# Letting attention steps wait for their PSUM bank in the clock model of a gated cross-attention and expert kernel

## The chip, the cores and the metric

The kernel runs on one core of a Trainium2 chip. The metric is the device time of one execution in microseconds (us), as the median of several executions. The profiler records one execution; its span runs from the first to the last recorded instruction, and the execution's own time is a little longer than its span. The engines are TensorE (PE, with its weight loads as PEld), VectorE (DVE), ScalarE (ACT), GpSimd (POOL) and SyncE (SP), which here only issues DMAs and waits.

## The reference

Four batches of 2048 rows of width 512 go through two gated layers. `context` has 128 rows for each batch. Everything is in float32.

```python
def layernorm(x): return (x - mean(x)) / sqrt(var(x) + 1e-5)        # over the last axis

def xattn(query, ref):                                              # ref: 128 rows
    Q, K, V = query @ Wq + bq, ref @ Wk + bk, ref @ Wv + bv
    return (softmax(Q @ K.T) / sqrt(512)) @ V

def ffn(x):                                                         # one expert for a batch
    e = argmax(mean(x, rows) @ Wr + br)                             # of 8
    return relu(x @ W1[e] + b1[e]) @ W2[e] + b2[e]                  # 512 -> 2048 -> 512

x = x + tanh(g_xattn) * xattn(layernorm(x), context)
x = x + tanh(g_ffn) * ffn(layernorm(x))
```

## The kernel before

**Attention.** Rows are taken in 16 blocks of 512, four for each batch. Since `Q @ K.T` is `layernorm(x) @ (Wq @ K.T)` plus a bias, the kernel makes `M = Wq @ K.T` and `V` once for each batch (`keys`, `values`), and a block needs `x @ M` alone. The generator `attention` issues one block in steps: row statistics on DVE and POOL (tiles `st`, `mv`, `ve`, `rstd`), the scores `psc` on PE, softmax on DVE and ACT (`sc`, `nmax`), transposes `pp`, then four products `pav` with `V` (L288). DVE adds each of these to the rows (L276, `added`). Statistics are made again, ACT normalises (`xT`, L303, after DVE's `shift`, L297), PE transposes the result in four pieces `pt` (L335), and ACT copies each of them out with a column sum (L322, `copied`). The sums go into the mean that picks the expert.

`pav` and `pt` alternate between two small pools of PSUM banks, `ps_a` and `ps_t`. Blocks 0 to 2 share pools with two banks each; block 3 and all blocks of later batches have one bank in each pool. So the third `pav` of a later block needs the bank of the first, which DVE's add gives back, and the third `pt` needs ACT's first copy.

**Feed-forward.** Each layer's product is cut into quarters twice and done with 7 products in place of 8 at either level (49 in place of 64); the sums of blocks that this needs are made by DVE and POOL. For the weights they are made once for each batch and half of the hidden width: SP loads the expert's blocks (`base`, `home`, L593 and L599), POOL and in the first half also DVE sum them (L564), SP stores the sums to DRAM (`W1d`, `W2d`, L585), and a ring of four large and two small tiles `w` takes them back (L777 to L790). The first four groups of the first stage use the sums where they are made. There are 16 stages (4 batches, 2 pairs of blocks, 2 halves of the hidden width); all products are issued by `chain` (L811) into banks `X`, `Y` and `Q`.

**Who sets the order.** Nothing is reordered on the chip's queues by the program at run time: the order in which the Python code issues instructions is the order of each engine's queue. That order comes from generators and a clock model. A generator yields what its last instructions cost, as pairs such as `("DVE", 0.76)`. `Stream.step` adds these up. A step may yield two chains; the stream goes on at the end of the first one (`at`), and remembers the end of the latest in `later`. A step that yields the word `"join"` sets `at` to `later`.

The kernel has two parts. Up to the feed-forward (the prologue), the next stream is always the one with the smallest `at`, and a `filler` (`others`, the keys and values of batches 1 to 3) is put in wherever the model's PE is free before that. After it, the feed-forward's own steps call `tick`, which lets the stream `slow` (attention of later batches and their routing) and the stream `staged` (weight sums) take as many steps as a credit allows (`paced`, `PACE`), if their `at` is no more than 1.4 us ahead.

The steps of `pav` and `pt` yield two chains: PE's time, then the time of the add on DVE or the copy on ACT. The bank counter `held` is lowered when the add or copy is issued, not when the model has it done.

```python
            if t - 1 in pav:
                added(t - 1)
            yield (("PE", 0.87 * (t < 4)),), (("DVE", 0.76 * (t > 0)),)
```

Other places that matter: `route` (zm, zb, `pr` L521, `ei`, L539) picks a batch's expert and only then can SP load its weights; `begin` (L1302) are six small products of zeros on the feed-forward's banks, the first of that part; the last rows are stored by `store` (L1137), which is called by the table `after`.

Of the kernel before, what the change touches and what calls it, by code (L numbers as in the profile page):

```python
# [89 lines left out]
def flamingo(tc, ctx, x, xT, cxT, g_x, g_f, WqT, Wk, Wv, bqk, bv, Wr, br, W1, b1, W2, b2, out):  # L90
    nc = tc.nc
    B, N, H = x.shape
# [8 lines left out]
    Q = 2 * P  # L101
# [74 lines left out]
    def room(ps):  # L176
        while held[ps] == ROOM[ps]:
            yield (("DMA", 0.3),)
        held[ps] += 1
# [16 lines left out]
    def attention(b, blk, pools):  # L196
# [84 lines left out]
        for t in range(5):  # L281
            if t < 4:
                ps, tag = ((ps_a, "pa"), (ps_t, "pt"))[t % 2]
                if held[ps] == ROOM[ps] and t - 1 in pav:
                    added(t - 1)
                yield from room(ps)
                pav[t] = ps.tile([P, H], F32, tag=tag, name="pav"), ps
                nc.tensor.matmul(  # L288
                    pav[t][0], lhsT=pT[:, t * P : (t + 1) * P], rhs=Vb, start=True, stop=True
# [4 lines that stand above are left out]
# [33 lines left out]
        for kc in range(KC + 1):  # L327
            if kc < KC:
                ps, tag = ((ps_t, "pt"), (ps_a, "pa"))[kc % 2]
                if held[ps] == ROOM[ps] and kc - 1 in pt:  # L330
                    copied(kc - 1)
                yield from room(ps)
                pt[kc] = ps.tile([P, TB], F32, tag=tag, name="pt"), ps
                for t in range(4):
                    nc.tensor.transpose(  # L335
                        pt[kc][0][:, t * P : (t + 1) * P], z[:, t, kc * P : (kc + 1) * P], ident
                    )
            if kc - 1 in pt:
                copied(kc - 1)
            yield (("PE", 0.45 * (kc < KC)),), (("ACT", 0.8 * (kc > 0)),)  # L340
# [44 lines left out]
    if True:  # L385
        M0 = mvp.tile([P, KC, S], F32, tag="M", name="M_0")
        V0 = mvp.tile([P, H], F32, tag="V", name="V_0")
        ctxT0, KT0 = in_home(stp, "tt", (1, KC, S), (KC, S), n=21 * P)
        ctxTr = sp.tile([P, B - 1, KC, S], F32, name="ctxTr")
        w = {name: sp.tile([P, KC, H], F32, name=f"w{name}") for name in ("k", "q", "v")}  # L390
        bvb = sp.tile([P, H], F32, name="bvb")
        KTr, V3 = in_home(hp, "s2", (KC, (B - 1) * S), (H,))
        Ms = sp.tile([P, B - 1, KC, S], F32, name="Ms")
        Vs, ready_kv = {}, set()
        order = [(b, blk) for b in range(B) for blk in range(NBLK)][:EARLY]
        streams = [
            attention(*i, (*homes[n], *three) if n < 3 else one) for n, i in enumerate(order)
        ]
        nc.sync.dma_start(ctxT0, cxT[:, 0:1])
        for c in range(KC):  # L400
            nc.sync.dma_start(w["k"][:, :, c * P : (c + 1) * P], Wk[:, :, c * P : (c + 1) * P])
        with nc.allow_non_contiguous_dma(reason="bias"):
            nc.scalar.dma_start(bvb, bv.partition_broadcast(P))
        nc.sync.dma_start(w["q"], WqT)
        next(streams[0])
        nc.sync.dma_start(w["v"], Wv)
        nc.sync.dma_start(ctxTr, cxT[:, 1:B])

        def keys(cT, n, KT, M, pc_out):

            took = 0.43 * n + 0.02

            def sums(name, left, right):
                yield from room(ps_k)
                p = ps_k.tile([P, n, S], F32, tag="pk", name=name)
                for k in range(KC):
                    nc.tensor.matmul(  # L417
                        p, lhsT=left(k), rhs=right(k), start=k == 0, stop=k == KC - 1
                    )
                    if k % 2:  # L420
                        yield (("PE", took),)
                return p

            for m in range(KC):
                pk = yield from sums(
                    "pk", lambda k: w["k"][:, k, m * P : (m + 1) * P], lambda k: cT[:, :, k, :]
                )
                nc.vector.tensor_scalar(
                    KT[:, m, :], pk.rearrange("p n s -> p (n s)"), bqk_t[:, KC + m : KC + m + 1],
                    None, ALU.add,  # L430
                )
                held[ps_k] -= 1
                yield (("DVE", 0.5),)
            for kc in range(KC):
                pm = yield from sums(
                    "pm", lambda m: w["q"][:, m, kc * P : (kc + 1) * P], lambda m: KT[:, m, :]
                )
                nc.scalar.copy(M(kc), pm)
                held[ps_k] -= 1
                yield (("ACT", 0.5),)  # L440
            pc = yield from sums("pc", lambda m: bqk_t[:, m : m + 1].to_broadcast([P, P]), lambda m: KT[:, m, :])
            nc.scalar.copy(pc_out, pc.rearrange("p n s -> p (n s)"))
            held[ps_k] -= 1
            yield (("ACT", 0.5),)

        def values(cT, V):
            yield from room(ps_k)
            pv = ps_k.tile([P, H], F32, tag="pk", name="pv")
            for kc in range(KC):
                nc.tensor.matmul(  # L450
                    pv, lhsT=cT[:, kc, :], rhs=w["v"][:, kc, :], start=kc == 0, stop=kc == KC - 1
                )
                if kc % 2:
                    yield (("PE", 1.72),)
            nc.vector.tensor_tensor(V, pv, bvb, ALU.add)
            held[ps_k] -= 1
            yield (("DVE", 0.75),)

        def own():

            yield (("DMA", 11),)
            first_keys = keys(ctxT0, 1, KT0, lambda kc: M0[:, kc : kc + 1, :], cq[:, 0:S])
            for _ in range(12):
                yield next(first_keys)
            for m in range(KC):
                st = small.tile([P, 6], F32, tag="st", name="st", bufs=4)
                mq = small.tile([P, 2], F32, tag="mq", name="mq", bufs=2)
                nc.vector.bn_stats(st, w["q"][:, m, :])
                nc.vector.bn_aggr(mq, st)
                nc.vector.tensor_scalar(  # L470
                    w["q"][:, m, :], w["q"][:, m, :], mq[:, 0:1], None, ALU.subtract
                )
                yield (("DVE", 1.3),)
            yield from first_keys
            MV[0] = [M0, None]
            yield from values(ctxT0[:, 0], V0)
            MV[0][1] = V0

        def others():

            for lo, hi in ((1, 2), (2, B)):
                at = slice(lo - 1, hi - 1)
                yield from keys(
                    ctxTr[:, at], hi - lo, KTr[:, :, (lo - 1) * S : (hi - 1) * S],
                    lambda kc: Ms[:, at, kc, :], cq[:, lo * S : hi * S],
                )
                for b in range(lo, hi):
                    Vs[b] = V3 if b == 3 else sp.tile([P, H], F32, name=f"V_{b}")
                    yield from values(ctxTr[:, b - 1], Vs[b])
                    ready_kv.add(b)  # L490
                    if b > 1:
                        nc.sync.dma_start(Md[b], Ms[:, b - 1, :, :])
                        nc.sync.dma_start(Vd[b], Vs[b])
            yield from until(lambda: 1 in MV)

        def second_batch():

            yield from until(lambda: 1 in ready_kv and all((0, i) in done_at for i in range(NBLK)))
            Mb = mvp.tile([P, KC, S], F32, tag="M", name="M_1")
            Vb = mvp.tile([P, H], F32, tag="V", name="V_1")  # L500
            nc.scalar.copy(Mb, Ms[:, 0])
            nc.scalar.copy(Vb, Vs[1])
            MV[1] = [Mb, Vb]
            yield (("ACT", 1.2),)
# [232 lines left out]
    NS = B * NF * 2  # L737
# [213 lines left out]
    Ys = {}  # L951
# [165 lines left out]
    def ffn2(b, blk, fh, half):  # L1117
# [15 lines left out]

        def store(cp, i):
            if fh:
                o = slice(2 * cp, 2 * cp + 2)
                nc.sync.dma_start(rows(out, b, 2 * blk + i)[:, o, :], Ys[i][:, o, :])  # L1137

        def add(cp, j, v):
            i, m = divmod(j - 11, 10)  # L1140
# [27 lines left out]
        def both(j, cp):  # L1168
# [6 lines left out]
            (2, 0): [(s4, 0), (both, 21, 0)], (2, 1): [(s4, 1), (both, 22, 0)],  # L1175
            (5, 0): [(both, 21, 1)], (5, 1): [(both, 22, 1)],
            (4, 0): [(store, 0, 1), (bias, 0)], (4, 1): [(store, 1, 1)],
            (3, 0): [(store, 0, 0)], (3, 1): [(store, 1, 0)],
        }
        groups = group(0), group(1)  # L1180
        for q in ORDER2:
# [21 lines left out]
    ctx.enter_context(tc.manual_schedule())  # L1203


    BUSY = {"PE": 1.0, "DVE": 1.3, "ACT": 1.3, "POOL": 1.0, "DMA": 1.1, "Q": 1.1, "POW": 4.0, "GAP": 1.0}

    class Stream:
        def __init__(self, gen, at):
# [196 lines left out]
```

## Time and profile before

| | us |
|---|---|
| median of 3 executions (1743.45 to 1746.9) | 1745.74 |
| the profiled execution's own time | 1742.86 |
| its span | 1741.1 |
| PE busy in the span | 1686.3 (97%) |
| DVE, POOL, ACT busy | 1048.7, 654.6, 581.9 |
| `begin` waits, then the feed-forward starts at | 121.9 |
| last add of `y` on DVE starts at | 1736.82 |

A line of instructions gives the start, the busy time, engine, line, operation, `out<-in`, forms and count, and in square brackets the engine's idle time before it with what ended that idle time. A line of stretches gives the stretch, its length, the busy time of PE, PEld, DVE, ACT and POOL with the number of instructions, then PEclk, the share of full TensorE clock that was granted, and DMA use. A line of waits gives who waited for whom, the sum, how often, and the longest.

### The profile page before, as it was taken

Reading aid. Unit: us, or ns where it says so; the run is one execution under the profiler, and the core shown is the slowest. Engines: PE = TensorE matmul, PEld = TensorE weight load, DVE = VectorE, ACT = ScalarE, POOL = GpSimd, SP = SyncE. Lnnn points to the kernel's source line nnn. Section 1 sums busy time; section 2 is a strip of 40 time slices with the busy share of each in tenths; the row PEclk is TensorE's granted clock in tenths of the full one; section 3 lists DMA queues with packets and bytes.
Section 4 is the critical chain, followed back from the end, with each engine's and each line's share of the span. In section 5 each row is a group of like instructions: output and inputs, shape, how many; then the busy total and the mean of one; then the engine's idle time right before and its main releaser. Section 6 shows DMA issues by size and latency. Waiting matters only on the chain.

```text
span 1741.1 us, 21919 instructions
## 1 busy us (share of the span) xinstructions
PE 1686.3 (97%) x7965; PEld 1439.3 (83%) x7966; DVE 1048.7 (60%) x1663; ACT 581.9 (33%) x1284; POOL 654.6 (38%) x536
## 2 busy tenths in 40 slices
PE   6889999999999999998999999999999999999999
PEld 5667788888888888787878788888888888888887
DVE  5756576556666674757648565583846464746362
ACT  1524225253251614514144252322323242414150
POOL 0365424420648621366156520576514210331010
PEclk8989999999999999999999999999999999999999
DMA  7267777465687965478769564679744543545242
GB/s 296 97 255 287 280 259 287 157 237 190 247 324 259 356 235 178 156 284 299 288 244 344 193 229 142 228 276 318 292 150 155 164 160 101 180 145 174 91 136 80
DMA packets 143067, 381.87 MB, mean 219 GB/s; under 512 B 10480, under 2 KB 40176, under 8 KB 128624
## 3 DMA queue, kind: packets, MB, share of 16 engines
q1 hardware_dynamic: 136912, 342.43, 55.9%
q10 hardware_dynamic: 6048, 38.04, 5.5%
q8 instruction: 64, 1.05, 0.2%
q14 instruction: 43, 0.35, 0.1%
HBM read 262.99 MB, written 117.44 MB: 219 GB/s over the span
## 4 chain that ended last, share of the span: by engine, by line
PE 86%; DVE 6%; DMA 4%; issue 1%; ACT 1%; POOL 1%; SPq 0%; DVEq 0%; POOLq 0%; ACTq 0%
PE Y L811 34%; PE Q L811 23%; PE X L811 21%; DMA w<-W1d 3%; PE pav L288 2%; PE psc L234 2%; PE pt L335 1%; DVE st L214 1%; DMA home<-in_W_dram 1%; PE pm L417 1%; PE pv L450 1%; DVE x L276 1%; DVE c L1009 1%; PE pk L417 0%; DMA wq<-in_WqT_dram 0%
## 5 line engine op out<-in xcount | busy, mean ns | idle before, releaser
L811 PE MATMUL Y<-z,w 128*128 128x256 f32 x1296 | 322.8, 382 | 18.0 <-DMA w<-W1d 8.8
L811 PEld LDWEIGHTS Y<-z,w 128*128 128x128 f32 x1296 | 242.7, 190 | 65.2 <-DVE Q L1063 12.8
L978 ACT ACTIVATE h<-c,b1T 128x256 f32<-128x256 f32 x512 | 229.5, 500 | 86.8 <-DVE c L1009 37.1
L564 POOL TENSOR_TENSOR base<-base 128x512 f32<-128x512 f32 (+1 forms) x126 | 183.5, 1462 | 175.5 <-DMA base<-in_W_dram 171.2
L830 ACT COPY Y<-X 128x512 f32<-128x512 f32 x144 | 82.2, 571 | 467.6 <-PE X L811 467.2
L811 PE MATMUL Y<-w,h 128*128 128x256 f32 x1024 | 228.8, 380 | 0.0
L811 PE MATMUL X<-w,h 128*128 128x256 f32 x1024 | 227.9, 379 | 0.0
L811 PE MATMUL Q<-w,h 128*128 128x256 f32 x1024 | 226.9, 379 | 0.0
L811 PEld LDWEIGHTS X<-w,h 128*128 128x128 f32 x1024 | 193.9, 190 | 29.0 <-issue 3.1
L811 PEld LDWEIGHTS Y<-w,h 128*128 128x128 f32 x1024 | 194.7, 191 | 28.1 <-issue 2.0
L811 PEld LDWEIGHTS Q<-w,h 128*128 128x128 f32 x1024 | 194.3, 190 | 26.2
L811 PE MATMUL Q<-z,w 128*128 128x256 f32 x864 | 212.1, 385 | 1.3
L811 PE MATMUL X<-z,w 128*128 128x256 f32 x864 | 207.4, 379 | 0.0
L811 PEld LDWEIGHTS Q<-z,w 128*128 128x128 f32 x864 | 164.8, 193 | 28.6 <-issue 4.2
L1000 POOL TENSOR_TENSOR r<-r,cg 128x512 f32<-128x512 f32 x32 | 40.6, 1270 | 390.3 <-DVE cg L1081 388.4
L811 PEld LDWEIGHTS X<-z,w 128*128 128x128 f32 x864 | 163.5, 190 | 24.8 <-issue 3.3
L564 POOL TENSOR_TENSOR z<-z 128x256 f32<-128x256 f32 x156 | 129.0, 851 | 37.4 <-DVE z L564 33.6
L220 POOL TENSOR_TENSOR rstd<-ve,mhalf 128x4 f32<-128x4 f32 x32 | 34.9, 1089 | 279.1 <-DVE ve L219 279.0
L811 PE MATMUL Y<-w,s 128*128 128x256 f32 x512 | 113.6, 379 | 0.0
L1142 DVE SCALAR_TENSOR_TENSOR y<-Y,gf,y 128x512 f32<-128x512 f32 x64 | 47.8, 746 | 103.1 <-PE Y L811 101.9
L811 PEld LDWEIGHTS Y<-w,s 128*128 128x128 f32 x512 | 96.8, 190 | 12.9
L1142 DVE SCALAR_TENSOR_TENSOR y<-X,gf,y 128x512 f32<-128x512 f32 x32 | 23.9, 746 | 135.3 <-issue 70.7
(145 smaller groups left out, 2081.9 us busy)
## 6 DMA issues: line engine op xcount, KB each, us to landing
w<-W1d SPq DMA_DIRECT2D x108, 512.0 KB, 4.3
w<-W1d SPq DMA_DIRECT2D x108, 384.0 KB, 4.4
w<-W2d SPq DMA_DIRECT2D x64, 512.0 KB, 7.2
base<-in_W_dram SPq DMA_DIRECT2D x29, 1024.0 KB, 8.5
W1d<-base SPq DMA_DIRECT2D x14, 1792.0 KB, 9.3
w<-in_W_dram SPq DMA_DIRECT2D x48, 512.0 KB, 5.1
W1d<-tt SPq DMA_DIRECT2D x14, 1344.0 KB, 6.0
xT<-in_xT_dram SPq DMA_DIRECT2D x16, 1024.0 KB, 10.9
```

What stands on the lines that cost most here:

```text
L214: nc.vector.bn_stats(st, xt[:, t, :])
L220: nc.gpsimd.tensor_tensor(rstd, ve, mhalf, ALU.pow)
L234: nc.tensor.matmul(psc[:, t, :], lhsT=xTt[:, kc, t * P : (t + 1) * P], rhs=Mb[:, kc, :], start=kc == 0, stop=kc == KC - 1,)
L276: nc.vector.scalar_tensor_tensor(xt[:, t, :], t_, coef[:, t : t + 1], xt[:, t, :], ALU.mult, ALU.add)
L288: nc.tensor.matmul(pav[t][0], lhsT=pT[:, t * P : (t + 1) * P], rhs=Vb, start=True, stop=True)
L335: nc.tensor.transpose(pt[kc][0][:, t * P : (t + 1) * P], z[:, t, kc * P : (kc + 1) * P], ident)
L564: eng.tensor_tensor(o, l, r, ALU.subtract)
L811: nc.tensor.matmul(bank[:, c, :], lhsT=left(k, c), rhs=right(k, c), start=fresh and c == 0 and k == 0, stop=c == 1 and k == ks - 1, skip_g ...
L830: nc.scalar.copy(t["Y"], t["X"])
L978: nc.scalar.activation(h[ij][:, v, 2 * m + c, :], src[:, c, :], AF.Relu, bias=b1T[:, f + c : f + c + 1],)
L1000: eng.tensor_tensor(r[j], r[j], v, ALU.add)
L1142: nc.vector.scalar_tensor_tensor(o, v, gf, o, ALU.mult, ALU.add)
```

## The change

Three places, and numbers in a table.

1. In `attention`, the third and fourth `pav` and the third and fourth `pt` are preceded by a `"join"`: in the model, the step that needs a bank back goes on only when the add or copy that was issued before it is done. On the chip the instructions stay the same; their place in the queues moves. Each block has four steps more.
2. In `keys`, the copy of a piece of `M` out of PSUM is issued on ACT or DVE, whichever the model has free first.
3. In the last stage, the rows that are finished last are stored in two column halves. The left columns are stored ahead of the others by the new `store_left`.
4. In the table `BUSY`, factors for DVE, ACT and POW are other numbers.

```diff
@@ attention
                 if held[ps] == ROOM[ps] and t - 1 in pav:
                     added(t - 1)
+                if t > 1:
+                    yield "join"
                 yield from room(ps)
                 pav[t] = ps.tile([P, H], F32, tag=tag, name="pav"), ps
...
                 if held[ps] == ROOM[ps] and kc - 1 in pt:
                     copied(kc - 1)
+                if kc > 1:
+                    yield "join"
                 yield from room(ps)
                 pt[kc] = ps.tile([P, TB], F32, tag=tag, name="pt"), ps
@@ keys
-                nc.scalar.copy(M(kc), pm)
+                name = min(("ACT", "DVE"), key=lambda n: free[n])
+                (nc.scalar.copy if name == "ACT" else nc.vector.tensor_copy)(M(kc), pm)
                 held[ps_k] -= 1
-                yield (("ACT", 0.5),)
+                yield ((name, 0.5),)
@@ ffn2
         def store(cp, i):
             if fh:
-                o = slice(2 * cp, 2 * cp + 2)
-                nc.sync.dma_start(rows(out, b, 2 * blk + i)[:, o, :], Ys[i][:, o, :])
+                o, c = slice(2 * cp, 2 * cp + 2), slice(Q * (s == NS - 1 and i == 0), H)
+                nc.sync.dma_start(rows(out, b, 2 * blk + i)[:, o, c], Ys[i][:, o, c])
+
+        def store_left(cp):
+            if s == NS - 1:
+                o, c = slice(2 * cp, 2 * cp + 2), slice(0, Q)
+                nc.sync.dma_start(rows(out, b, 2 * blk)[:, o, c], Ys[0][:, o, c])
...
-            (3, 0): [(store, 0, 0)], (3, 1): [(store, 1, 0)],
+            (3, 0): [(store_left, 0), (store_left, 1), (store, 0, 0)], (3, 1): [(store, 1, 0)],
@@ the clock model
-    BUSY = {"PE": 1.0, "DVE": 1.3, "ACT": 1.3, "POOL": 1.0, "DMA": 1.1, "Q": 1.1, "POW": 4.0, "GAP": 1.0}
+    BUSY = {"PE": 1.0, "DVE": 1.0, "ACT": 1.0, "POOL": 1.0, "DMA": 1.1, "Q": 1.1, "POW": 1.5, "GAP": 1.0}
```

As built, the changed program has the same matrix products. Three of the twelve copies of `M` pieces move from ACT to DVE, four sums of `z` blocks (128x256) move from DVE to POOL, and two stores are added. The order of the queues is another one from the first `pav` on, in the prologue and in nearly every attention block after it.

## The prediction

> **What bounds the kernel now.** I read the page first, then busy time by stretch, then who PE waits for in each stretch, then the queues around the waits.
>
> ```profile
> 0.00:28.00 28.00, 14.39 (x75) 13.48 (x76) 12.35 (x33) 2.81 (x8) 1.86 (x9) 0.82 0.90 334
> 28.00:122.00 94.00, 83.33 (x426) 61.00 (x426) 67.76 (x156) 34.03 (x97) 39.47 (x34) 0.95 0.42 163
> 122.00:185.00 63.00, 56.49 (x249) 47.06 (x247) 36.38 (x57) 27.31 (x61) 36.69 (x25) 0.92 0.84 321
> 185.00:1737.00 1552.00, 1532.13 (x7220) 1317.77 (x7220) 931.60 (x1419) 517.72 (x1119) 576.60 (x469) 1.00 0.62 217
> 1737.00:1741.10 4.10, 0.00 (x0) 0.00 (x0) 0.56 (x1) 0.00 (x0) 0.00 (x0) 0.91 0.31 128
> ```
>
> PE is the bound, and its work does not change. What can be won is idle time and slow clock: 13.6 us idle up to 28, 10.7 in the prologue from 28 to 122, 6.5 from 122 to 185, 19.9 in the remaining 1552 us, 4.1 at the end. The column PEclk adds 0.05 x 94 = 4.7 us of lost clock in the prologue and 0.08 x 63 = 5.0 after it.
>
> PE's waits from 28 to 122, then from 185 to 1737:
>
> ```profile
> PE pv L450 <- ACT Ms L438: 2.9, 1, 2.9
> PE begin L1302 <- DVE home L455: 2.8, 1, 2.8
> PE pr L521 <- DVE zb L515: 2.1, 1, 2.1
> ```
>
> ```profile
> PE Y L811 <- DMA w<-W1d: 5.3, 4, 2.1
> PE Y L811 <- DVE Q L1063: 4.6, 6, 2.1
> PE pav L288 <- DVE x L276: 3.7, 2, 3.1
> PE pt L335 <- ACT x L322: 2.9, 8, 0.4
> ```
>
> The change aims at the last two lines and at the prologue's queue order. The prologue's three waits, on PE and on the engine it waits for:
>
> ```profile
> 76.11 1.06 PE L417 MATMUL pc<-home,bqk_t 128*128 128x128 f32 x8
> 80.10 5.40 PE L450 MATMUL pv<-wv,ctxTr 128*128 128x512 f32 x8 [2.93 <-ACT Ms L438]
> 95.28 1.85 PE L521 MATMUL pr<-wr,zb 128*128 128x8 f32 x8 [2.14 <-DVE zb L515]
> 118.70 0.38 PE L1302 MATMUL begin<-zero 128*128 128x512 bf16 x1
> 121.90 1.33 PE L1302 MATMUL begin<-zero 128*128 128x512 bf16 x4 [2.82 <-DVE home L455]
> ```
>
> ```profile
> 78.38 1.52 ACT L303 ACTIVATE xT<-x,shift,rstd 128x512 f32<-128x512 f32 x2 [1.87 <-DVE shift L297]
> 91.45 0.48 DVE L428 TENSOR_SCALAR home<-pk,bqk_t 128x256 f32<-128x256 f32 x1 [3.15 <-PE pk L417]
> 94.23 0.90 DVE L515 COPY zb<-zm 128x512 f32<-128x512 f32 x1
> 115.86 5.38 DVE L564 TENSOR_TENSOR tt<-base,tt 128x896 f32<-128x896 f32 x2
> 121.17 0.68 DVE L455 TENSOR_TENSOR home<-pv,bvb 128x512 f32<-128x512 f32 x1
> ```
>
> ACT, in queue order, holds `Ms` behind `xT`, which waits for block 3's `shift`: PE has nothing from 77.17 to 80.10, and runs the next eight `pv` in 5.40 us, where 3.45 is usual. ACT's last copy of `pt` ends at 90.7, but DVE stands before the `home` copy that waits for PE until 91.45, then makes `z` sums, so `zb` is ready only at 95.13. From `zb` hang the expert's number, the loads of its weights (issued at 99.98), DVE's sums of them, and behind these sums, in DVE's queue, the last `V`, for whose bank `begin` waits until 121.9.
>
> **Part by part.** *The prologue's joins.* I follow the new queue orders with the durations of these rows. Up to DVE's first `coef` (42.5) all is as before, and DVE is full from 36 to 68. From there to block 3's `shift` its work is 33.6 us less 1.75 idle, plus 0.25 for an `Ms` copy: 32.1. In the new order I count some 3.7 us of waits on it (0.3 for `psc`, 1.0 for `pav` of block 1, 1.2 for block 2's fourth `pav`, which stands behind `pp` of block 3, 1.2 for the last `rstd`), so `shift` starts at 78.3, against 76.04. It took 2.30 us before, beside POOL's first `z` sum, and that sum again starts with it: 80.6 against 78.35. But ACT has by then done all of blocks 0 and 1 and three of four `xT` of block 2; left are 5 `xT` (0.75), one small copy and 8 copies of 0.58: 89.2 against 90.7. PE waits some 2 us for block 2's last `xT`, as it waited 2.93.
>
> Behind the last copy DVE now has `zm` and `zb` at once, since only the first half of the `home` copies stands ahead and its products are issued before the last `pt`: `zb` at 90.9 in place of 95.13. The loads go out 4.5 to 5 us after the `pr` products and the seven small steps to `ei`, as before: 94.5 against 99.98. The eight `base` sums follow 5.5 us after that; then come DVE's three `tt` (1.5, 2.7, 2.7), `base` (2.4), four `z` (0.7 each) and two `V` (0.6): the last `V` at 116.8 against 121.85. PE itself is through with `pv` at 110.4 by its work, so it waits 6 us there and starts slow, as before. **Term: -5.1.** Bounds: if DVE's chain did not hold, PE's own work would allow 112 with some slow clock, -9; if ACT's or DVE's waits cost 5 us more than I counted, nothing is won, 0.
>
> *From 122 to 185.* Two waits, 2.8 on DVE and 3.6 on a weight load, end a chain of DMAs and POOL sums that starts with the routing; DMA use is 0.84. It moves with the loads, by 5.5 against the 5.1 above: **0**, bounds -2 and +3.
>
> *The joins in later blocks.* After `begin`, three `pav` in a row stand six times in the old order and never in the new one (four in a row twice in both); runs of 12 or 16 pieces of `pt` fall from 8 to 3. The 3.1 us wait at 965.6 is such a third `pav`, behind DVE's queue of `y` and `h`. It goes (-3.1; the other one, 0.6, mostly too), five of eight waits of `pt` go (-1.8), and the slow clock behind 968 (3.4 us at half, -1.7). What is late next: DVE's adds come later by one product, and the block's end too. The four further steps use up credit, so attention falls back by up to 8 weight loads of 21 a stage, in the last batch. That batch's last weight sums are stored 4 loads ahead of its first one; its first half, which is needed first, over 20 ahead: no loss. But the stores of sums, which hold SP until POOL is done and then load the DMAs, now stand at other places ahead of `w` loads. Before, three weight waits near 2 us and one slow stretch came of this. I take one more such wait with a slow stretch (2.1 + 1.7): +3.8. **Term: -6.6 + 3.8 = -2.8 or so, rounded to -3.** Bounds: -8 and +8 (a wait in each of three more places).
>
> The clock, by the rows of 4 us: after PE's wait at 77 it is 0.69 and 0.88, after that at 93 0.50 and 0.75, after 119 0.57. A wait of 2 us or more cost about its own length again.
>
> [...]
>
> *The last stores.* SP issues the last store at 1737.6 and the span ends 3.5 us later. It becomes 256 KB, and the left half goes out before. Rows of 256 KB land in 3.6 to 5.2, the 512 KB stores in 4.7 (2.6 at least): from +0.5 to -1.7 (half of 3.5); I take **-0.5**.
>
> [...]
>
> *The rest at nothing.* Of the `M` copies, the one in the first keys fills DVE's wait for rows from 22.9 to 25.9, and ACT did it in 0.27; without that cover 0.3. Four `z` sums on POOL (0.85 each, DVE 0.54) lie ahead of `home` sums that wait for a load; without that, 3 us on the chain of W1d stores. `BUSY` is read only for engines other than DVE, ACT and POOL, no step yields POW, and the other factors are equal: this edit moves nothing.
>
> Sum: -5.1 + 0 - 3 - 0.5 = **-8.6**: 1742.86 becomes 1734.3. The profiled execution lies 2.9 below the median of the three, so the median should be 1737.1.
>
> **Rivals.** *No change (0.18).* The prologue stays where it is: DVE loses in the new order, with two blocks' `pav` and `pt` between each other, what the routing wins, and later waits cancel. For it: DVE ends later by my own count, and 10.7 us idle is what remains of 94. Against it: `zb` lost 4.4 us to a queue order that is gone. Sum near -1: 1745.
>
> *Slower (0.20).* SP's queue decides. A store of sums waits on SP for POOL (up to 10.2 us at a time before), then puts 3.1 MB in front of the next weight; that landed in 9.9 us at 779, where 4.3 is usual, and PE waited 2.1. The ring hides about 8 us of hold; from there each us is PE's. Attention's later steps put `rstd` and stores elsewhere on POOL and SP; five further waits of 2.1 with slow clock 1.7 are +19, less the prologue's 5 and 5 of the `pav` and `pt`: +9, 1754.
>
> *Joins without effect in later blocks (part of the first case).* Then -5.6 remains: 1740.
>
> **How the numbers follow.** A measurement of this kernel tells about 0.2% (3.5 us) from no change. My case: 0.62, from 1729 to 1742, at 1737. No change: 0.18. Slower: 0.20, 1749.3 to 1760. Cutting off the far half of the slower case and a tenth below gives 1729 to 1750.
>
> **What would show it.** Right: `begin` starts the feed-forward near 117, `zb` ends near 91, the wait `pv <- Ms` is gone or a `pt <- xT` of 2 us stands in its place, `begin <- home` is longer than 2.8; from 185 on `pav <- x` below 1 us; the tail about 0.5 shorter. Wrong: `begin` later than 120, weight waits (`Y <- w`) over 12 us, or a new slow stretch in each batch.

## The result, and the profile after

The changed kernel takes 1755.13 us (median of four executions, 1754.15 to 1757.18) against 1744.6 for the kernel before: 10.5 us more. The recorded ratio is 1.0069, with an interval of 1.0053 to 1.0085; it is not the quotient of these two medians, 1.0060, and by it the loss is some 12 us. The profiled execution took 1755.2, with a span of 1753.4, against 1742.86 and 1741.1.

Stretches of the changed kernel first, cut where those of before were cut (columns as there):

```profile
28.00:122.00 94.00, 86.22 (x447) 63.30 (x446) 68.66 (x151) 35.47 (x98) 45.89 (x39) 0.96 0.47 181
122.00:185.00 63.00, 55.78 (x244) 46.03 (x243) 39.47 (x64) 25.36 (x58) 33.29 (x24) 0.92 0.83 318
185.00:1737.00 1552.00, 1517.36 (x7145) 1308.18 (x7145) 930.50 (x1408) 517.37 (x1118) 580.39 (x469) 0.99 0.61 215
1737.00:1753.40 16.40, 12.44 (x58) 10.62 (x56) 3.28 (x5) 0.00 (x0) 0.00 (x0) 0.99 0.35 129
```

The prologue is better: PE does 86.2 us of work from 28 to 122, where it did 83.3. The long stretch is worse: PE is idle for 1552 - 1517.4 = 34.6 us of it, where it was 19.9, and the clock falls from 1.00 to 0.99. PE's waits in the feed-forward say for what (185 to the end):

```profile
PE Y L817 <- DMA w<-W1d: 24.9, 5, 7.2
PE pav L291 <- DVE x L276: 3.7, 5, 1.0
PE Y L817 <- DVE Q L1069: 2.8, 3, 1.4
PE pt L340 <- ACT x L325: 1.1, 3, 0.4
```

Weights from `W1d` cost 24.9 us, not 5.3. The wait of `pav` is cut into five short ones, but its sum is the same 3.7; that of `pt` falls from 2.9 to 1.1. Four of the weight waits are long: 6.9 at 571.4, 3.7 at 606.3, 7.2 at 1200.3 and 4.0 at 1234.9; the fifth is 3.1. This is the one at 1200.3 as PE sees it:

```profile
1198.42 1.89 PE L817 MATMUL X<-z,w 128*128 128x256 f32 x8
1207.55 2.04 PE L817 MATMUL Y<-z,w 128*128 128x256 f32 x4 [7.24 <-DMA w<-W1d]
1209.38 3.62 PE L817 MATMUL Q<-z,w 128*128 128x256 f32 x8
```

Eight products of 256 columns take 1.89 us ahead of the wait and 3.62 behind it, where the granted clock is 0.50 (1207.5 to 1211). SP's queue shows where the weight was. First the changed kernel, then the one before, at the same place of the feed-forward:

```profile
1184.66 0.33 SPq L1143 DMA_DIRECT2D out_dram<-y  x1
1195.48 0.57 SPq L591 DMA_DIRECT2D W1d<-tt  x1
1197.53 0.55 SPq L591 DMA_DIRECT2D W1d<-base  x1
1198.17 2.62 SPq L796 DMA_DIRECT2D w<-W1d  x2
1201.06 1.09 SPq L605 DMA_DIRECT2D base<-in_W_dram  x1
1202.24 19.34 SPq L796 DMA_DIRECT2D w<-W1d  x5
```

```profile
1198.04 0.89 SPq L790 DMA_DIRECT2D w<-W1d  x2
1200.55 0.57 SPq L585 DMA_DIRECT2D W1d<-tt  x1
1202.60 0.56 SPq L585 DMA_DIRECT2D W1d<-base  x1
1204.09 6.92 SPq L790 DMA_DIRECT2D w<-W1d  x4
```

Before, two weight loads went out ahead of the store of sums and the first landed in 3.8 us (1201.86). In the changed kernel both stand behind the store, and the store waits for POOL's sums `tt`: SP issues nothing from 1185.0 to 1195.5. Then 1344 and 1792 KB of stores go out, and the first weight lands 9.2 us after its issue, at 1207.41, one us after the second store (1206.36). Two stretches of the changed kernel show the same in DMA use (the last but one column):

```profile
1184.00:1196.00 12.00, 12.00 (x57) 10.43 (x56) 4.68 (x7) 5.44 (x10) 11.84 (x12) 1.00 0.32 100
1196.00:1207.50 11.50, 4.31 (x20) 3.44 (x19) 2.06 (x3) 4.25 (x9) 1.50 (x1) 0.83 0.96 342
```

While SP is held the DMA engines stand at 0.32 and POOL is at work for 11.84 of 12 us; then they run at 0.96 and PE waits. Near 571 the store stands behind the same 82 weight loads as before, but POOL's sums end at 559.9 in place of 557.7 while PE is 4 to 5 us ahead of where it was. SP's wait for `tt` there is 6.6 us, before 0.9; then it waits 2.4 for that store to land, since the next load goes into the same tile, and the weight behind it lands 12.6 us after its issue. POOL is late because a block that it sums ahead of these comes 5 us later (the row of before first):

```profile
511.81 5.31 POOL L564 TENSOR_TENSOR base<-base 128x512 f32<-128x512 f32 x4 [17.02 <-DMA base<-in_W_dram]
516.86 7.77 POOL L570 TENSOR_TENSOR base<-base 128x512 f32<-128x512 f32 x4 [24.74 <-DMA base<-in_W_dram]
```

After that block POOL works on without a pause up to 559.9. The store of sums ahead of the block's load stands behind 72 weight loads, not 68; the load waits for that store to land and now follows four loads of `z`, which came behind it before.

### The profile page after: what moved, and what is told of

The parts are those of the page before. It is cut to its first block, busy times and chain, and to the rows that moved or that the text cites. A ratio compares the mean times of both kernels' runs of the same rounds, so it can differ in the third digit from the quotient of the medians.

```text
span 1753.4 us, 21910 instructions
## 1 busy us (share of the span) xinstructions
PE 1688.1 (96%) x7966; PEld 1443.2 (82%) x7966; DVE 1055.4 (60%) x1662; ACT 581.0 (33%) x1281; POOL 661.4 (38%) x540
## 3 DMA queue, kind: packets, MB, share of 16 engines
q8 instruction: 64, 1.05, 0.2%
## 4 chain that ended last, share of the span: by engine, by line
PE 86%; DVE 5%; DMA 5%; POOL 1%; ACT 1%; issue 1%; SPq 0%; DVEq 0%; POOLq 0%; ACTq 0%
PE Y L817 33%; PE Q L817 22%; PE X L817 22%; DMA w<-W1d 4%; PE psc L234 3%; PE pav L291 3%; PE pt L340 1%; DMA home<-in_W_dram 1%; PE pk L422 1%; DVE c L1015 1%; PE pm L422 1%; DVE y L1154 1%; DVE st L214 1%; DVE cg L1087 0%; DVE x L276 0%
## 5 line engine op out<-in xcount | busy, mean ns | idle before, releaser
L817 PE MATMUL Y<-z,w 128*128 128x256 f32 x1296 | 329.4, 388 | 34.9 <-DMA w<-W1d 27.8
L817 PEld LDWEIGHTS X<-z,w 128*128 128x128 f32 x864 | 163.4, 190 | 25.6 <-issue 3.8
L570 POOL TENSOR_TENSOR z<-z 128x256 f32<-128x256 f32 x159 | 135.3, 873 | 29.0 <-DVE z L570 24.1
L817 PEld LDWEIGHTS Y<-w,s 128*128 128x128 f32 x512 | 96.7, 190 | 12.8
L1057 ACT COPY s<-Q 128x512 f32<-128x512 f32 x112 | 65.2, 582 | 97.1 <-PE Q L817 93.9
```

What stands on the lines that cost most here:

```text
L570: eng.tensor_tensor(o, l, r, ALU.subtract)
L817: nc.tensor.matmul(bank[:, c, :], lhsT=left(k, c), rhs=right(k, c), start=fresh and c == 0 and k == 0, stop=c == 1 and k == ks - 1, skip_g ...
L1057: nc.scalar.copy(t, v)
```

## The experiments

**What the runs are measured by.** Beside the ratio to the kernel before, the table gives four readings of each profiled execution: the start of the 211th of the 6720 feed-forward products (the prologue and what its lead is still worth), the time from there to the last product, PE's idle time in it, and the sum of `Y`'s waits for `W1d` after 185.

| run | ratio (interval) | 211th product | to the last | idle | W1d waits |
|---|---|---|---|---|---|
| before | 1 | 188.1 | 1548.7 | 19.7 | 5.3 |
| the change | 1.0069 (1.0053 to 1.0085) | 182.9 | 1566.6 | 34.6 | 24.9 |
| e1, joins, prologue | 1.0042 (1.0025 to 1.0059) | 187.6 | 1552.2 | 22.2 | 4.6 |
| e2, joins, later | 1.0104 (1.0090 to 1.0119) | 186.5 | 1565.6 | 35.1 | 25.6 |
| e3, joins free of credit | 0.9978 (0.9967 to 0.9989) | 182.9 | 1548.2 | 19.3 | 5.5 |
| e4, no joins | 0.9967 (0.9954 to 0.9980) | 184.2 | 1549.5 | 20.3 | 6.5 |
| e5, M copies alone | 0.9971 (0.9958 to 0.9983) | 183.8 | 1546.4 | 18.6 | 4.6 |
| e6, credit 1.06 | 1.0082 (1.0063 to 1.0101) | 187.8 | 1562.5 | 32.0 | 18.0 |
| e7, credit 1.10 | 1.0099 (1.0079 to 1.0119) | 186.6 | 1567.6 | 31.7 | 15.8 |
| e8, stores from POOL | 1.0061 (1.0040 to 1.0083) | 185.3 | 1562.5 | 33.5 | 23.9 |
| e9, SP not held | 0.9971 (0.9955 to 0.9986) | 183.1 | 1547.4 | 22.1 | 12.7 |
| e10, prologue, all | 0.9970 (0.9955 to 0.9985) | 182.7 | 1548.3 | 18.9 | 4.6 |
| e11, no joins, credit 1.4 | 1.0043 (1.0029 to 1.0056) | 181.0 | 1558.4 | 29.5 | 14.6 |
| e12, joins, credit 1.4 | 1.0107 (1.0082 to 1.0132) | 182.4 | 1568.4 | 34.6 | 15.2 |
| e13, no joins, SP not held | 1.0046 (1.0028 to 1.0063) | 181.5 | 1561.4 | 28.8 | 14.8 |
| e14, credit 1.06, SP not held | 1.0009 (0.9997 to 1.0021) | 186.3 | 1549.7 | 22.5 | 12.8 |
| e15, base2 later | 1.0022 (1.0008 to 1.0036) | 182.9 | 1555.6 | 27.3 | 18.2 |

**Which part of the change.** Four runs take it apart. e1 and e2 have only the joins, in one half of the program each:

```diff
-                if t > 1:
+                if t > 1 and ahead_of_ffn[0]:          # e1; e2: not ahead_of_ffn[0]
                     yield "join"                       # the same for kc > 1
```

> Joins only in the prologue; M copies on ACT and stores as before. Theory (the loss comes from the joins in the later blocks: each takes a step of credit, routing of batches 2 and 3 comes 2 and 7 weight loads later, and the stores of weight sums then hold SP ahead of weight loads): begin near 115, no wait of Y for W1d over 2.5 us after 185, 1744.6 - 5.2 = about 1739. Rival (PE now starts 6 us early and POOL's sums do not come earlier with it, so SP's stores are late by themselves): waits of 6 to 7 us near 571 and 1200 as in the changed kernel, 1752 to 1756.

> Joins only in the blocks after begin; all else as before. Theory: begin at 121.9 as before, the two places of long weight waits are there (over 15 us of Y <- w in all after 185), 1744.6 + 12.3 + 5.2 = about 1762, at least 1755. Rival (the early start is needed for the waits): 1741 to 1747, and the waits of pav gone.

e2 came as the theory says: 1.0104, with both places of long waits (6.9 at 575, 6.8 at 1205). So the early start is not needed for the loss. e1 has no such waits, as expected, but it is slower too, which neither side expected. Its `zb` is ready at 91.6, and it starts the feed-forward 8.1 us earlier, but it has 0.5 left at the 211th product: PE waits 7.0 for a `w` at 136.8 and 5.1 for a `pav` at 176.8. At 294.9 it waits 4.5 for a W2 weight that stands behind a W2d store and four loads of `z`; in the order of before the `z` loads come some weight loads later.

e3 keeps all joins, but a join after `begin` uses no credit; e4 has none:

```diff
             due[name] -= 1
             if not stream.step():
                 stream = None
+            elif joined[0]:            # e3: the step was a "join"
+                due[name] += 1
```

> The changed kernel, but a join after begin takes no credit from the stream. Order of SP's queue: the sums' stores and routings stand again behind the same number of weight loads as before. Theory: no long weight waits, begin near 115, the wait of 3.1 us for a pav gone: 1735 to 1740. Rival (the joins' own new order of PE, DVE and ACT makes the loss, not the credit): 1750 or more.

> No joins: only the M copies on the freer engine and the last rows stored in two column halves. Both theories: within 0.2% of before, the end about 0.4 shorter (tail 3.9 against 4.3), 1741 to 1746.

Both are faster than before. The line of e3 that decides:

```profile
PE Y L817 <- DMA w<-W1d: 5.5, 4, 2.3
PE pav L291 <- DVE x L276: 3.3, 2, 2.7
```

With the joins in place and their credit given back the long weight waits are gone, 19.4 us of them; so it is not the joins' order on PE, DVE and ACT that costs. Nor does that order gain: the long `pav` wait is still there (2.7), and e3 is no faster than e4. e4 was expected within 0.2% of before and is 0.33% faster: a miss. e5 and e10 ask where that came from:

```diff
-                nc.scalar.copy(M(kc), pm)                       # e5: this edit alone
+                name = min(("ACT", "DVE"), key=lambda n: free[n])
+                (nc.scalar.copy if name == "ACT" else nc.vector.tensor_copy)(M(kc), pm)
```

> No joins, stores as before: only the M copies on the freer engine. If the 5 us that the run without joins gained come from M copies that no longer stand behind ACT's xT (zb near 90.6 in place of 95.1): ratio near 0.997, about 5 us less the 0.4 of the tail. If they come from the stores by columns: 1.000, a tail of 4.3 with begin at 121.9.

> Joins in the prologue only, M copies on the freer engine and stores by columns as in the changed kernel. If the run with the joins alone lost its time to SP's order from 122 to 300 (stores of sums ahead of the first weight loads, z loads ahead of a W2d load), which with the copies on the freer engine is that of before again: 1735 to 1740, ratio near 0.997, as with the copies alone, so the prologue's joins add nothing. If prologue joins cost by themselves: 1743 or more. If they gain beside the copies: under 1734.

The copies alone give 0.9971. `zb` in e5, on DVE:

```profile
89.72 0.91 DVE L521 COPY zb<-zm 128x512 f32<-128x512 f32 x1
```

and in the changed kernel, with the last `V` sum:

```profile
88.98 0.90 DVE L521 COPY zb<-zm 128x512 f32<-128x512 f32 x1
114.33 0.68 DVE L461 TENSOR_TENSOR home<-pv,bvb 128x512 f32<-128x512 f32 x1
```

So the prologue's gain, `zb` at 89.9 or 90.6 in place of 95.1, needs no join: a copy of `Ms` on DVE no longer stands behind ACT's `xT`. The joins alone bring `zb` to 91.6 as well (e1), but there the lead is lost on the way. With the copies in place the prologue's joins change nothing that can be told: the 211th product begins at 182.7 in e10 and 184.2 in e4, and runs with the same order up to `begin` differ by 2.9 there; the times agree. The stores by columns shorten the tail by 0.4 (4.31 to 3.92); between e4 and e5 that can't be told from noise.

**Is it the credit alone?** e6 and e7 are the kernel before with one number changed:

```diff
-    PACE = {"slow": (3.,1.2,1.2), ...}
+    PACE = {"slow": (3.,1.06,1.06), ...}        # e6; e7: 1.10
```

> The kernel before with one number changed: the credit of the later attention is 1.06 steps in place of 1.2. No joins, no copies moved. By SP's order it puts routing of batches 2 and 3 behind 121 and 187 weight loads (before 119 and 182; changed kernel 121 and 189) and stores of sums behind 72, 198, 208 (before 68, 187, 200; changed kernel 72, 198, 208). Theory (lost credit alone makes the loss): long waits of Y for W1d near 575 and 1205, ratio 1.008 to 1.012. Rival (the joins' order on PE, DVE and ACT makes it): ratio 1.000 to 1.002.

> As the run with 1.06, with a credit of 1.10: the store of sums behind 68 loads moves to 72 as there, but routing of batch 2 stays behind 119 and that of batch 3 moves by 2 only (184), the later stores by none or two. Theory: the wait near 575 is there (6 to 7 us, and one of 3.5 some 35 us later), those near 1205 are not: ratio 1.003 to 1.007. Rival: 1.000.

```profile
PE Y L811 <- DMA w<-W1d: 18.0, 6, 5.9
```

e6 brings the loss back without any join, with waits of 5.9 at 577 and 4.4 at 1208. SP's waits for POOL's `tt` and `base` sums after 185 go the same way: 104.8 us before, 147.9 in the changed kernel, 145.2 in e6, 103.3 in e3. e7 was a miss in place and size: no wait above 3.5, but nine of them for `W1d`, 5.7 us for `pav`, and 1.0099. A smaller loss of credit costs as much, elsewhere. e11 and e12 give more credit, 1.4, without and with the joins:

> No joins, M copies on the freer engine, stores by columns, and the credit of the later attention at 1.4 in place of 1.2. By SP's order routings come one weight load earlier at most and stores of sums move by one load. If less credit costs because attention then comes late, more credit does no harm: 1733 to 1740, waits of pav and of weights after 185 no longer than in the run without joins; a gain of up to 4 us if the wait of 3.1 us for a pav goes. If any other order than the tuned one costs: 1745 or more.

> The changed kernel with the credit at 1.4, so that the joins' four steps in each block are paid for by more steps. By SP's order routing of batches 2 and 3 is behind 119 and 182 weight loads again, the stores of sums where they were before. Theory (credit): no wait of 6 to 7 us near 571 and 1200, 1735 to 1742. Rival: 1750 or more.

Both missed the theory as I had written it. In e12 the long waits near 571 and 1200 are gone and the stores of sums stand where they were, but there are seven waits for `W1d` up to 3.5, and `pt` waits 8.5 us for ACT (2.9 before): 1.0107. e11 has 8.9 there and 14.6 for `W1d`, and takes 0.8% more than e4, the same kernel with 1.2 (1.0043 against 0.9967; its profiled execution, 1745.1, is the fastest of its twelve, so the table's row shows rather less than the median's loss). Less credit costs and more credit costs, and SP's order counted in weight loads does not foretell the time by itself.

**What turns the order into waits.** e8 issues the stores of W1d sums from POOL's queue, behind the sums; e9 also moves the next load into their tile, `base2`; e15 does only that:

```diff
-        nc.sync.dma_start(dst, src)                    # e8, e9: put() of W1d in stage_half
+        nc.gpsimd.dma_start(dst, src)
...
-                yield (("DMA", 7),)                    # e9, e15
+                yield (("DMA", 10),)
                 t = second_tile(k)
```

> The changed kernel, but the stores of the W1d sums of stage_half are issued from POOL's queue behind the sums themselves, not from SP's. SP is not held by them; the bytes and about the same time of the stores stay. Theory A (SP's hold, 6.6 and 10.2 us, keeps the weight loads behind it back): the waits near 571 and 1200 fall below 2.5 us, 1736 to 1742, if POOL's issuing costs it little. Theory B (the 3.1 MB themselves are in the weights' way): the waits stay above 4 us, 1750 or more.

> The changed kernel with two edits in stage_half: the stores of the W1d sums are issued from POOL's queue, and the next load into their tile (base2), which in the run before still held SP until the store had landed, stands some four weight loads later in SP's queue. Now nothing holds SP ahead of the weight loads near 571; the bytes are the same. Theory A (SP held behind the sums): the waits near 571 and 606 are gone (below 2 us each), 1740 to 1748. Theory B (the bytes of stores and base loads are in the way): waits of 5 us and more stay there, 1750 or more.

> The changed kernel with only one of the two edits: base2's load three model microseconds later, behind four weight loads; the stores of sums stay on SP and hold it for POOL's sums (6.6 us near 560). If the landing behind the store (3.8 us) is what counts: no wait over 2.5 us near 571, ratio 0.997 to 1.001. If the hold for POOL's sums counts: a wait of 3 us or more near 571 and 1.004 or more.

e8 could not tell its two theories apart: SP was held all the same, from 555.9 to 567.2, by the `base2` load, which waits until the store from its tile has landed. In e9 no store of W1d sums holds SP, and the changed kernel falls from 1.0069 to 0.9971, with its joins and its lost credit:

```profile
PE Y L817 <- DMA w<-W1d: 12.7, 5, 8.7
```

That is faster than the 1740 to 1748 I expected (1736.0). The wait at 571 is 1.7, and 0.5 is left near 1210; but a wait of 8.7 stands at 599, where I expected none above 2. It is of the same kind: SP waits 6.5 us for POOL ahead of a store of W2 sums, which I had not moved; that store goes out at 591.5, two loads of `y` (1 MB each) behind it, and only then the weight, at 593.4, which lands at 607.3. So theory A holds at 571 and at both places near 1200; at 606 another hold of the same kind took the wait's place. e15 lies between (1.0022): neither side had that. The wait near 571 is 1.1, though SP still waits 5.8 for POOL's sums ahead of it; the one at 598 is 8.6, and at 1200 one of 5.4 stays. So near 571 the landing counts, and near 1200 probably the hold for the sums as well. The last two runs ask whether a free SP cures the kernel in general:

> No joins, M copies on the freer engine, stores by columns, and SP not held as in the run before: stores of the W1d sums from POOL's queue, the base2 load some weight loads later. If SP's holds also cost the kernel without joins: 1730 to 1734, ratio 0.993 to 0.996. If they are hidden there: 1736 to 1739, 0.997.

> The kernel before with a credit of 1.06 (which cost 1.008 by itself) and SP not held. If SP's holds turn late sums into waits: ratio 0.996 to 1.002. If less credit costs in other ways: 1.006 or more.

e14's time is as expected: credit 1.06 costs 1.0082 with SP held and 1.0009 without. e13 does not: without joins, at the tuned credit, the same edit costs 0.8% (1.0046 against e4's 0.9967), with waits of 7.9 at 597 (again behind a store of W2 sums, issued at 589.9, and the loads of `y`) and 3.4 at 1232. It is no cure; it makes another order, with other meetings of stores and weights. All four runs with `base2` later (e9, e13, e14, e15) have one wait of 7.9 to 9.2 near 600.

## Why the prediction was wrong

- **The later blocks, "-6.6 + 3.8, rounded to -3"**: this term failed. From the 211th product to the last the time grew by 17.9 us (1548.7 to 1566.6): PE's idle time by 15.0, and what PE lost to the half clock while at work by 5.9 (9.3 against 3.4); 3 us the other way are not assigned. Of the -6.6, the sum of `pav` did not move (five waits of up to 1.0 in place of two); the 1.8 of `pt` came, and so did the 1.7, for no slow stretch follows 968 now. Of the +3.8, "one more such wait" was four, and the sum grew by 19.6 us. Its base was misread too: before had two weight waits near 2 us, not three (2.1, 1.9, then 0.8), and the slow stretch at 815 follows a wait of 2.1 for DVE's `Q`. The steps of credit and the later routing came as counted (7 loads later in the last batch). The mistake was the question: I asked whether sums would be ready for their own stage ("over 20 ahead: no loss"), and not how long SP would stand at their stores while other stages' weights were due. Near 1200 the store came two weight loads earlier than before; near 571 it kept its place, and POOL was late.
- **The rival "SP's queue decides"** named the mechanism and, at 1754, nearly the time, with 0.20. It assumed five waits of 2.1; there were four of 3.7 to 7.2 at two places and one of 3.1. "The ring hides about 8 us of hold" was too kind: a hold of 6.6, with 2.4 for a landing, cost 6.9, and one of 10.4 cost 7.2, since the stores behind a hold then delay the weight too (12.6 and 9.2 us to land).
- **The prologue, -5.1**: right in size, and right from `zb` on. `zb` ended at 89.9 (90.9 predicted), the loads went out at 94.62 (94.5), the last `V` ended at 115.0 (116.8), the feed-forward began 6.3 us earlier and kept 5.2 at the 211th product. Ahead of `zb` there was luck: `shift` ended at 76.6 (80.6 predicted) and ACT's last copy of `pt` at 86.7 (89.2), but one of DVE's `z` sums then took 2.6 us. `begin` waited 2.8, not 6. I also put the `M` copies at nothing, and e5 shows that they suffice; the joins alone (e1) move `zb` too, but keep only 0.5.
- **From 122 to 185, 0**: +1.1. **The last stores, -0.5**: -0.4.
- **What would show it**: the sign for wrong, "weight waits over 12 us", is what the profile shows, 24.9. Of the signs for right, `pav <- x` below 1 failed (3.7), and `pt <- xT` is 0.5, not 2.
- **The clock around `begin`**: in the traces of before and of the change, the stretches at a clock of 0.50 inside the runs last 3.41, 6.83 or 10.24 us. Around `begin`'s wait of 2.8 there was one of 3.41 in either kernel (from 122.5 before, from 114.6 in the change), as in the sum; around the wait of 7.6 in e3 one of 10.24, from 116.7 on (e3's clock is 0.94 from 28 to 122 and 0.96 from 122 to 185).

What stays open: why a credit of 1.10 costs as much as the joins, and one of 1.4 costs with and without them. SP waits longer for POOL's sums in two of these runs, 123.0 us in e7 and 129.3 in e12 against 104.8 before, but not in e11 (107.1). Their losses are spread over many waits of 1 to 5 us, and no run here takes those apart.

## What to carry to other kernels

A step that costs the chip nothing can cost a hand-made scheduler its credit: count the steps that a change adds, and what falls back by them. Here a store that waited for POOL's sums held SP, and the loads behind it, from 1185.0 to 1195.5, and the weight behind it then landed 9.2 us after its issue, 3.8 before the change; look at what stands behind each store, not only at when its data are needed. Of a change with several parts, run each part alone: here the smallest edit, the copy on the freer engine, gives 0.997 of before by itself, which no other run beats measurably, and the joins of the later blocks lose 1.0% by themselves.

## What the runs showed of the hardware

- What the prologue gained could not be read at its end. Seven runs with one and the same order up to `begin` waited there 2.8 us (the change, e9), 3.6 (e12), 6.3 (e10, e15) or 7.6 (e3, e8), since DVE's sums took longer in some (its last sums of `z` and `base` 0.94 and 1.60 us in the change, 2.29 and 2.95 in e3); yet the 211th product began at 182.4 to 183.1 in six of these seven, 185.3 in e8.
- Near 1200 a weight of 384 KB behind 3.1 MB of stores landed 9.2 us after its issue, at 1207.41, 1.05 us after the store ahead of it; before the change, ahead of the stores, 3.8.
